# Layer 1's attention beside message passing: values scaled on their way out of PSUM, keys' squares summed by ScalarE, and the step cut in three

## The chip, the cores and the metric

The kernel runs on one core of a Trainium2 chip. The metric is the device time of one execution in microseconds. Three runs of the kernel before took 2911.58, 2914.35 and 2914.36 us; their median is 2914.35 us.

## What is computed

A two-layer graph network on 3125 nodes with 256 features and 50000 edges. Layer 1 adds two branches to x: an edge-softmax message passing, and an attention whose softmax is absent, so that its products can be regrouped. The two branches concerned, cut to what matters and written as plain formulas:

```
xn  = layernorm(x)                                  # 3125 x 256
# branch 1, per edge e = (src, dst), 4 heads of 64
msg = d0[e] * (xn[src] @ Wf.T) + d1[e] * (xn[src] @ Wr.T)      # 64 values
s   = leaky_relu(msg . attn[h], 0.2)                           # 4 scores
out[dst, h] = sum_e softmax_dst(s)[e, h] * msg
# branch 2, 8 heads of 64
k, v = instance_norm(xn @ Wk.T), instance_norm(xn @ Wv.T)      # over each head's 64
out  = (q @ (k.T @ v) / 3125) @ Wout.T + bout
x    = x + branch1 + branch2
```

## The kernel before

`layer1_mix` does branch 1 in a loop over groups of 8 columns of 128 edges: 391 columns, so G = 49 groups, and G + 2 = 51 steps of the loop, numbered i = 0 to 50. The PSUM has eight banks and all are given out: 2 for `ln_pt` (pool `ps_a`), 1 for `pdots`, 4 for `pw` (pool `ps_w`), 1 for `psm`.

What step i issues, in this order:

- `messages(i)` (L1206 to L1217): VectorE weighs the gathered rows by direction, makes scores and their maxima `mx`; TensorE transposes `mx`.
- `weigh(i-1)` (L1263): VectorE multiplies 8 x 4 x 64 message values by the exponentials of the group before. The exponentials lie in column 64 of the tile `v` in SBUF, written by ScalarE (L1238).
- `maximum(i)` (L1224 to L1230): VectorE reduces the transposed maxima, TensorE transposes the new maximum back.
- `products(i-1)` (L1271): TensorE multiplies one-hot matrices with `v`, two or three node tiles of each group, each in a `pw` bank. The profile counts each of these fp32 products as two instructions; there are 14 to 32 of them in a step.
- `add(i-2)` (L1280 to L1287): VectorE adds the products of the group before to `acc`; ScalarE makes the first copy of a node tile.
- `ones_of(i)` (L1255) and `exponents(i)` (L1235 to L1240): one-hot matrices on VectorE, then the subtraction of the maximum and ScalarE's exponentials.
- `next(todo)`: one piece of branch 2, out of the generator `galerkin`.

`galerkin`'s pieces fall on the steps as follows. Step 0 has the weights `wkv`. Steps 1 to 26 have t = 0 to 25: for the tile t-1 VectorE reduces the squares (L1457), forms the product of the variances (L1458, L1460), ScalarE takes its root (L1461), VectorE the reciprocal (L1462), and VectorE scales the values (L1463); TensorE adds keys times values to `pdots` (L1465). Then TensorE makes keys and values of tile t in two `ln_pt` banks (L191), ScalarE copies both out (L1475) and squares both (L1477). Step 27 has `dots` and `woT`, step 28 `m2`, step 29 the matrix `g` and the first chunk of tiles, steps 30 to 35 the other six chunks (L1514, L1515), each of 4 or 3 tiles.

The order is written by hand: TensorE, VectorE and ScalarE run their instructions in the order of the program (`manual_schedule`), each engine waiting on its own for what it needs. GpSimd issues the gathers three groups ahead.

Of the kernel before, what the change touches and what calls it, by code (L numbers as in the profile page):

```python
# [8 lines left out]
F32 = mybir.dt.float32  # L9
I32 = mybir.dt.int32  # L10
BF16 = mybir.dt.bfloat16
AF = mybir.ActivationFunctionType
OP = mybir.AluOpType
AX = mybir.AxisListType
PSUM = bass.MemoryType.PSUM
# [3 lines left out]
D = 256  # L19
P = 125  # L20
# [5 lines left out]
GROUP = 8  # L26
# [23 lines left out]
def gather(nc, out, table, idx):  # L50
    nc.gpsimd.indirect_dma_start(  # L51
        out=out, out_offset=None, in_=table,
        in_offset=bass.IndirectOffsetOnAxis(ap=idx, axis=0))
# [35 lines left out]
class Kernel:  # L89
# [1063 lines left out]
    def layer1_mix(self):  # L1153
        nc, tc, a = self.nc, self.tc, self.a
        W, HD = 68, 64
        with ExitStack() as m:
            big = m.enter_context(tc.tile_pool(name="l1", bufs=1))
            wk = m.enter_context(tc.tile_pool(name="l1w", bufs=2))
            gp = m.enter_context(tc.tile_pool(name="l1g", bufs=3))
            ps_a = m.enter_context(tc.tile_pool(name="l1pa", bufs=2, space=PSUM))  # L1160
            ps_c = m.enter_context(tc.tile_pool(name="l1pc", bufs=1, space=PSUM))
            ps_w = m.enter_context(tc.tile_pool(name="l1pw", bufs=4, space=PSUM))
            ps_s = m.enter_context(tc.tile_pool(name="l1ps", bufs=1, space=PSUM))

            xT = big.tile([128, 2, N], F32, name="xT2")
# [3 lines left out]
            for t0, n in CHUNKS:  # L1169
                st = wk.tile([P, 4, 2 * W], F32, name="t1_st")  # L1170
                for i in range(n):
                    pm = ps_a.tile([P, 2 * W], F32, name="ln_pt")
# [22 lines left out]
            def fetch(j0):  # L1195
                n = min(GROUP, NJ - j0)
                g = gp.tile([128, GROUP, 2 * W], F32, name="g1", bufs=4)
                for i in range(n):
                    gather(nc, g[:, i, :], tab1[:], self.t_src[:, j0 + i:j0 + i + 1])
                return j0, n, g  # L1200
# [32 lines left out]
            def exponents(n, s, pb):  # L1233
                big2 = gp.tile([128, 2, 4], F32, name="top_b", bufs=4)
                nc.vector.tensor_copy(big2, pb)  # L1235
                nc.vector.tensor_sub(s[:, :n, :], s[:, :n, :], big2[:, 0:1, :].to_broadcast([128, n, 4]))
                v = gp.tile([128, GROUP, 4, HD + 1], F32, name="v1", bufs=2)
                nc.scalar.activation(v[:, :n, :, HD], s[:, :n, :], AF.Exp)  # L1238
                grown = gp.tile([128, 4], F32, name="grown", bufs=4)
                nc.scalar.activation(grown, big2[:, 1, :], AF.Exp)  # L1240
                return big2, grown, v

            def tiles_in(j0, n):

# [5 lines left out]
            def ones_of(j0, n):  # L1250

                hots = []
                for w, i0, k in tiles_in(j0, n):
                    hot = gp.tile([128, GROUP, P], F32, name="hot", bufs=5)
                    nc.vector.scalar_tensor_tensor(  # L1255
                        hot[:, :k, :], self.t_dst[:, j0 + i0:j0 + i0 + k, None].to_broadcast([128, k, P]),
                        float(-w * P), self.node[:, None, :P].to_broadcast([128, k, P]),
                        op0=OP.add, op1=OP.is_equal)
                    hots.append(hot)
                return hots  # L1260

            def weigh(n, o, v):
                nc.vector.tensor_mul(v[:, :n, :, :HD], o[:, :n, None, :HD].to_broadcast([128, n, 4, HD]),  # L1263
                                     v[:, :n, :, HD:].to_broadcast([128, n, 4, HD]))

            def products(j0, n, v, hots):
                sums = []
# [23 lines left out]
            with tc.manual_schedule(engines={E_.PE, E_.DVE, E_.Activation}):  # L1291
                todo = self.galerkin(big, wk, ps_a, ps_c, xT)
                starts = [(j0, min(GROUP, NJ - j0)) for j0 in range(0, NJ, GROUP)]
                G = len(starts)
                ahead = [fetch(starts[i][0]) for i in range(3)]
                msg, exps, summed = {}, {}, {}
                for i in range(G + 2):
                    if i + 3 < G:
                        ahead.append(fetch(starts[i + 3][0]))
                    if i < G:  # L1300
                        j0, n, g = ahead[i]
                        o, s, pt = messages(j0, n, g)
                    if 0 <= i - 1 < G:
                        weigh(starts[i - 1][1], msg[i - 1][0], exps[i - 1][2])
                    if i < G:
                        pb = maximum(pt)
                    if 0 <= i - 1 < G:
                        summed[i - 1] = products(*starts[i - 1], exps[i - 1][2], msg[i - 1][1])
                    if 0 <= i - 2 < G:
                        add(*starts[i - 2], *exps[i - 2][:2], summed[i - 2])  # L1310
                    if i < G:
                        msg[i] = o, ones_of(j0, n)
                        exps[i] = exponents(n, s, pb)
                    next(todo, None)
                last = exps[G - 1][0]
# [14 lines left out]
            for t0, n in CHUNKS:  # L1330
                s = slice(t0, t0 + n)
                for t in range(t0, t0 + n):
                    for h in range(4):
                        xs = self.x[:, t, h * HD:(h + 1) * HD]
# [93 lines left out]
    def galerkin(self, big, wk, ps_a, ps_c, xT):  # L1428

        nc, a = self.nc, self.a
        wkv = big.tile([128, 2, 1024], F32, name="wkv")
        for c4 in range(2):
            nat = wk.tile([128, 4, D], F32, name="nat4", bufs=1)
# [16 lines left out]
        kvs = {}  # L1452
        for t in range(NT + 1):
            if t > 0:
                kv, sq = kvs.pop(t - 1)
                var = wk.tile([P, 16], F32, name="kv_var")
                nc.vector.tensor_reduce(var, sq, AX.X, OP.add)  # L1457
                nc.vector.tensor_scalar(var, var, 1.0 / 64, LN_EPS, op0=OP.mult, op1=OP.add)  # L1458
                both = wk.tile([P, 8], F32, name="kv_both")
                nc.vector.tensor_mul(both, var[:, 0:8], var[:, 8:16])  # L1460
                nc.scalar.activation(both, both, AF.Sqrt)  # L1461
                nc.vector.reciprocal(both, both)  # L1462
                nc.vector.tensor_mul(kv[:, 8:, :], kv[:, 8:, :], both[:, :, None].to_broadcast([P, 8, 64]))  # L1463
                for hp in range(4):
                    nc.tensor.matmul(pc[:, hp, :],  # L1465
                                     kv[:, 8 + 2 * hp:10 + 2 * hp, :].rearrange("p a b -> p (a b)"),
                                     kv[:, 2 * hp:2 * hp + 2, :].rearrange("p a b -> p (a b)"),
                                     start=(t == 1 and hp == 0), stop=(t == NT and hp == 3),
                                     skip_group_check=True)
            if t < NT:  # L1470
                kv = wk.tile([P, 16, 64], F32, name="kv")
                for i in range(2):
                    pk = ps_a.tile([P, 512], F32, name="ln_pt")
                    self.token_matmul(pk, xT, t, wkv[:, :, 512 * i:512 * i + 512])
                    nc.scalar.copy(kv[:, 8 * i:8 * i + 8, :].rearrange("p a b -> p (a b)"), pk)  # L1475
                sq = wk.tile([P, 16, 64], F32, name="kv_sq", bufs=1)
                nc.scalar.activation(sq, kv, AF.Square)  # L1477
                kvs[t] = kv, sq
            yield
        dots = big.tile([128, 4, 128], F32, name="dots")  # L1480
        nc.vector.memset(dots, 0.0)
        for s in (slice(0, 64), slice(64, 128)):
            nc.vector.tensor_copy(dots[s, :, s], pc[s, :, s])

        woT = big.tile([128, 4, D], F32, name="woT")
        nat = wk.tile([128, 2, 512], F32, name="nat4", bufs=1)
        nc.sync.dma_start(nat, a["L1_mix_Wout"].rearrange("(c p) f -> p c f", p=128))
        for cc in range(2):
# [2 lines left out]
                nc.tensor.transpose(pt[:, i, :], nat[:, cc, i * 128:(i + 1) * 128], self.ident)  # L1491
            nc.scalar.copy(woT[:, :, cc * 128:(cc + 1) * 128], pt)
        yield
        m2 = big.tile([128, 4, D], F32, name="m2")
        for hp in range(4):
            pm = ps_a.tile([128, D], F32, name="ln_pt")
# [2 lines left out]
        wq = wk.tile([128, 4, D], F32, name="nat4", bufs=1)  # L1499
        nc.sync.dma_start(wq, a["L1_mix_Wqkv"][0:512, :].rearrange("(c p) d -> p c d", p=128))  # L1500
        yield
        g = big.tile([128, 2, D], F32, name="gm")
        for k in range(2):
            pm = ps_a.tile([128, D], F32, name="ln_pt")
            for hp in range(4):
                nc.tensor.matmul(pm, wq[:, hp, k * 128:(k + 1) * 128], m2[:, hp, :],
                                 start=(hp == 0), stop=(hp == 3))
            nc.scalar.copy(g[:, k, :], pm)
        bout = self.bcast(big, "L1_mix_bout")
        for t0, n in CHUNKS:  # L1510
            for t in range(t0, t0 + n):
                pm = ps_a.tile([P, D], F32, name="ln_pt")
                self.token_matmul(pm, xT, t, g)
                nc.vector.tensor_add(self.x[:, t, :], self.x[:, t, :], pm)  # L1514
            nc.vector.tensor_add(self.x[:, t0:t0 + n, :], self.x[:, t0:t0 + n, :],  # L1515
                                 bout[:, None, :].to_broadcast([P, n, D]))
            yield


# [309 lines left out]
```

## Time and profile before

| view | what | value |
|---|---|---|
| runs | median of three | 2914.35 us |
| profiled execution | own time, span | 2909.29 us, 2907.5 us |
| page, part 1 | PE, VectorE, ScalarE, GpSimd busy | 75%, 53%, 17%, 57% of the span |
| windows | steps 2 to 26, 1653.2 to 1957.9 us | 304.7 us: PE 275.7, VectorE 270.8, ScalarE 136.9, GpSimd 242.4 busy; granted clock 0.99 |
| windows | steps 29 to 35, 1986.8 to 2116.9 us | 130.1 us: PE 85.2, VectorE 77.1, ScalarE 4.7, GpSimd 77.9 busy; clock 0.82 |
| windows | steps 36 to 50, 2116.9 to 2246.0 us | 129.1 us: PE 101.2, VectorE 114.0, ScalarE 7.4, GpSimd 86.2 busy; clock 0.87 |

A row of the timeline has the start in us, the duration in us, the engine, the line, the operation, its tiles (out<-in), shapes, a count of merged rows, and in brackets how long the engine sat idle before it and who ended that. PE is a matmul, PEld a weight load, DVE is VectorE, ACT is ScalarE, POOL is GpSimd. A row of a window table has the stretch, its length, and for each engine its busy time with the count of instructions, then the granted clock.

### The profile page before, as it was taken

The numbers are of one execution on the slowest core, as the hardware profiler recorded it, in microseconds if no ns is written. First come the engines' busy times: TensorE is split into PE (matmuls) and PEld (weight loads), VectorE is DVE, ScalarE is ACT, GpSimd is POOL, SyncE is SP. The second block draws the span as 40 slices with busy tenths as digits, with TensorE's granted clock in tenths as the row PEclk, the third lists the DMA queues.
The fourth block names the chain that finished last, engine by engine and source line by source line (L and its number), as shares of the span: only waits on it lengthen the run. The fifth ranks groups of instructions, "written<-read, shape, count | busy, mean of one in ns | idle before, by whom it ended". The sixth has DMA issues, their size and how long they took to land. (4 is left out here: it accounts for less than half of the span.)

```text
span 2907.5 us, 26381 instructions
## 1 busy us (share of the span) xinstructions
PE 2176.8 (75%) x9022; PEld 1642.5 (56%) x9022; DVE 1533.5 (53%) x3540; ACT 503.8 (17%) x1024; POOL 1645.7 (57%) x1489
## 2 busy tenths in 40 slices
PE   1761779999959999999994599886677669992600
PEld 1450557777645668888883466655555546661400
DVE  7975796644679212221115499886588412111337
ACT  2320000000012112222221244440000212220200
POOL 4888887770006316666661677777475077776040
PEclk9865879999959999999996799998888689996855
DMA  8921513342102135555544222222111211221214
GB/s 291 381 78 43 128 41 87 87 107 59 53 30 64 39 122 165 186 185 189 189 151 106 73 49 48 47 48 57 31 42 33 66 15 25 39 46 15 59 48 104
DMA packets 178958, 263.41 MB, mean 91 GB/s; under 512 B 54175, under 2 KB 143753, under 8 KB 175426
## 3 DMA queue, kind: packets, MB, share of 16 engines
q1 hardware_dynamic: 120432, 204.77, 22.8%
q0 software_dynamic: 52480, 47.70, 8.1%
q10 hardware_dynamic: 5894, 9.09, 0.9%
q8 instruction: 75, 1.23, 0.2%
q14 instruction: 77, 0.62, 0.1%
HBM read 177.13 MB, written 84.20 MB: 90 GB/s over the span
## 5 line engine op out<-in xcount | busy, mean ns | idle before, releaser
L58 POOL DMA_INDIRECT adj<-ch_sum,ch_place x391 | 500.3, 1280 | 152.0 <-issue 113.8
L51 POOL DMA_INDIRECT g<-tab,t_src x391 | 458.1, 1172 | 222.6 <-issue 111.9
L58 POOL DMA_INDIRECT sorted<-s_rows,pos x256 | 245.1, 957 | 187.0 <-DVE s_rows L1050 118.4
L460 PE MATMUL psum<-sup,adjT 125*125 125x256 f32 x1250 | 292.3, 394 | 46.6 <-DMA adjT<-adj 34.7
L1271 PE MATMUL pw<-v,hot 128*125 128x260 f32 x1244 | 318.5, 418 | 0.0
L460 PEld LDWEIGHTS psum<-sup,adjT 125*125 125x125 f32 x1250 | 240.3, 194 | 88.2 <-DMA adjT<-adj 25.3
L51 POOL DMA_INDIRECT G<-tabg,g_src x256 | 242.3, 947 | 80.0 <-issue 71.6
L1271 PEld LDWEIGHTS pw<-v,hot 128*125 128x125 f32 x1244 | 252.3, 206 | 47.3
L1626 PE MATMUL fpy<-fw,fh 128*125 128x256 f32 x800 | 183.4, 388 | 79.3 <-DVE fy L1628 52.7
L859 PE MATMUL ph<-xs,w 128*128 128x256 f32 x1024 | 231.3, 385 | 8.4 <-issue 6.8
L887 PE MATMUL py<-w,h 128*128 128x256 f32 x1024 | 231.2, 380 | 0.0
L859 PEld LDWEIGHTS ph<-xs,w 128*128 128x128 f32 x1024 | 193.9, 192 | 45.2 <-issue 18.6
L1626 PEld LDWEIGHTS fpy<-fw,fh 128*125 128x125 f32 x800 | 153.1, 192 | 112.6 <-DVE fy L1628 53.1
L887 PEld LDWEIGHTS py<-w,h 128*128 128x128 f32 x1024 | 192.5, 190 | 24.6
L861 ACT ACTIVATE h<-ph,b 128x256 f32<-128x256 f32 x256 | 121.2, 474 | 366.0 <-PE ph L859 336.5
L1618 PE MATMUL fph<-xT,fw 128*128 128x500 f32 (+1 forms) x448 | 174.5, 541 | 0.3 <-DMA fb<-in_L_ffn_b_dram 0.3
L1025 PE MATMUL pctx<-s_mv,s_ro 128*128 128x256 f32 x512 | 155.1, 414 | 1.9 <-DVE s_mv L1024 1.9
L1620 ACT ACTIVATE fh<-fph,cols 128x500 f32<-128x500 f32 (+1 forms) x112 | 70.6, 633 | 364.3 <-PE fph L1618 329.5
L890 DVE TENSOR_SCALAR yo<-py,own 128x256 f32<-128x256 f32 x64 | 29.6, 480 | 193.9 <-PE py L887 193.9
L58 POOL DMA_INDIRECT slots<-rows,abi x50 | 72.8, 1456 | 100.0 <-DVE r_cum L939 85.1
L463 DVE TENSOR_TENSOR x<-x,psum 125x512 f32<-125x512 f32 (+1 forms) x104 | 68.8, 664 | 108.9 <-PE psum L460 108.8
L1618 PEld LDWEIGHTS fph<-xT,fw 128*128 128x128 f32 x448 | 85.0, 191 | 72.6 <-issue 49.8
(495 smaller groups left out, 3241.2 us busy)
## 6 DMA issues: line engine op xcount, KB each, us to landing
adjT<-adj SPq DMA_DIRECT2D x25, 1367.2 KB
adj<-zero SPq DMA_DIRECT2D x22, 1536.0 KB
w<-in_L_ffn_W1p_dram SPq DMA_DIRECT2D x32, 1024.0 KB
w<-in_L_ffn_W2p_dram SPq DMA_DIRECT2D x32, 1024.0 KB
slots<-empty SPq DMA_DIRECT2D x1, 8448.0 KB
srow<-slots SPq DMA_DIRECT2D x32, 264.0 KB
adj<-ch_sum,ch_place POOLq DMA_INDIRECT x391, 4.4
g<-tab,t_src POOLq DMA_INDIRECT x391, 2.6
```

The lines of the kernel that those rows point to most:

```text
L51: nc.gpsimd.indirect_dma_start(out=out, out_offset=None, in_=table, in_offset=bass.IndirectOffsetOnAxis(ap=idx, axis=0))
L58: return nc.gpsimd.indirect_dma_start(out=table, out_offset=bass.IndirectOffsetOnAxis(ap=idx, axis=0), in_=rows, in_offset=None, **kw)
L460: nc.tensor.matmul(pm[:, i, :], mats[b][:, (a0 + i) * P:(a0 + i + 1) * P], sup[:, b, :], start=(b == b0), stop=(b == b0 + n - 1))
L463: nc.vector.tensor_add(xs, xs, pm[:, :m, :])
L859: nc.tensor.matmul(ph, w1[:, k, f * 128:(f + 1) * 128], xs[:, k, :], start=(k == 0), stop=(k == 1))
L861: nc.scalar.activation(h[:, f, :], ph, AF.Gelu, bias=b1[:, f:f + 1])
L887: nc.tensor.matmul(py, h[:, f, i * 128:(i + 1) * 128], w2[:, f, :], start=(f == 0), stop=(f == FC - 1))
L1025: nc.tensor.matmul(p1, ro[:, f - f0, :], mv, **st)
L1271: nc.tensor.matmul(pw.rearrange("p h c -> p (h c)"), hot[:, i - i0, :], v[:, i, :, :].rearrange("p h c -> p (h c)"), start=(i == i0), stop ...
L1618: nc.tensor.matmul(ph[:, :n * P], w1[:, k, f * 128:(f + 1) * 128], xT[:, k, t0 * P:(t0 + n) * P], start=(k == 0), stop=(k == 1))
L1620: nc.scalar.activation(hs[:, f, :n * P], ph[:, :n * P], AF.Gelu, bias=self.col("L1_ffn_b1", ei * FC + f))
L1626: nc.tensor.matmul(py, hs[:, f, i * P:(i + 1) * P], w2[:, f, :], start=(f == 0), stop=(f == FC - 1))
```

## The change

- `ScalarE` writes the exponentials twice: into a new PSUM tile `ev`, from which `weigh` reads them, and into `v` as before. `ev` takes one bank, so `pw` has 3 instead of 4.
- `galerkin`'s tile loop is cut in three by `yield`, and a step of the outer loop calls `next(todo)` three times: ahead of `messages`, ahead of `maximum`, and at the end. The first part holds the reduction of the squares up to the root, the second the reciprocal and the scaling, the third the products and the next tile's keys and values. The other pieces of `galerkin` are padded with empty parts so that they stay in their steps; `dots` comes in the first part of step 27.
- The values stay in PSUM; ScalarE scales them in eight copies by `both`. The keys' squares are summed by ScalarE in eight instructions with `accum_out`; the values are squared out of PSUM in one, and VectorE reduces 512 numbers instead of 1024.
- `bout` is a row added by a product with a row of ones, and two tiles are added to x at a time.

```diff
-            ps_w = m.enter_context(tc.tile_pool(name="l1pw", bufs=4, space=PSUM))
+            ps_w = m.enter_context(tc.tile_pool(name="l1pw", bufs=3, space=PSUM))
+            ps_e = m.enter_context(tc.tile_pool(name="l1pe", bufs=1, space=PSUM))
...
+                ev = ps_e.tile([128, GROUP, 4], F32, name="ev")
+                nc.scalar.activation(ev[:, :n, :], s[:, :n, :], AF.Exp)
                 nc.scalar.activation(v[:, :n, :, HD], s[:, :n, :], AF.Exp)
...
-                                     v[:, :n, :, HD:].to_broadcast([128, n, 4, HD]))
+                                     ev[:, :n, :, None].to_broadcast([128, n, 4, HD]))
...
+                    next(todo, None)
                     if i < G:
                         j0, n, g = ahead[i]
                         o, s, pt = messages(j0, n, g)
                     if 0 <= i - 1 < G:
-                        weigh(starts[i - 1][1], msg[i - 1][0], exps[i - 1][2])
+                        weigh(starts[i - 1][1], msg[i - 1][0], *exps[i - 1][2:])
+                    next(todo, None)
                     if i < G:
                         pb = maximum(pt)
...
+        yield
+        yield
         wkv = big.tile([128, 2, 1024], F32, name="wkv")
...
             if t > 0:
-                kv, sq = kvs.pop(t - 1)
-                var = wk.tile([P, 16], F32, name="kv_var")
-                nc.vector.tensor_reduce(var, sq, AX.X, OP.add)
+                kv, pv, var, sq = kvs.pop(t - 1)
+                nc.vector.tensor_reduce(var[:, 8:], sq, AX.X, OP.add)
...
                 nc.scalar.activation(both, both, AF.Sqrt)
+            yield
+            if t > 0:
+
                 nc.vector.reciprocal(both, both)
-                nc.vector.tensor_mul(kv[:, 8:, :], kv[:, 8:, :], both[:, :, None].to_broadcast([P, 8, 64]))
+                for h in range(8):
+                    nc.scalar.activation(kv[:, 8 + h, :], pv[:, 64 * h:64 * h + 64], AF.Copy,
+                                         scale=both[:, h:h + 1])
+            yield
+            if t > 0:
                 for hp in range(4):
...
             if t < NT:
                 kv = wk.tile([P, 16, 64], F32, name="kv")
-                for i in range(2):
-                    pk = ps_a.tile([P, 512], F32, name="ln_pt")
-                    self.token_matmul(pk, xT, t, wkv[:, :, 512 * i:512 * i + 512])
-                    nc.scalar.copy(kv[:, 8 * i:8 * i + 8, :].rearrange("p a b -> p (a b)"), pk)
-                sq = wk.tile([P, 16, 64], F32, name="kv_sq", bufs=1)
-                nc.scalar.activation(sq, kv, AF.Square)
-                kvs[t] = kv, sq
...
+                pk = ps_a.tile([P, 512], F32, name="ln_pt")
+                self.token_matmul(pk, xT, t, wkv[:, :, :512])
+                pv = ps_a.tile([P, 512], F32, name="ln_pt")
+                self.token_matmul(pv, xT, t, wkv[:, :, 512:])
+                for h in range(8):
+                    nc.scalar.activation(junk, pk[:, 64 * h:64 * h + 64], AF.Square,
+                                         accum_out=var[:, h:h + 1])
+                nc.scalar.copy(kv[:, :8, :].rearrange("p a b -> p (a b)"), pk)
+                nc.scalar.activation(sq.rearrange("p a b -> p (a b)"), pv, AF.Square)
+                kvs[t] = kv, pv, var, sq
             yield
...
         for t0, n in CHUNKS:
-            for t in range(t0, t0 + n):
-                pm = ps_a.tile([P, D], F32, name="ln_pt")
-                self.token_matmul(pm, xT, t, g)
-                nc.vector.tensor_add(self.x[:, t, :], self.x[:, t, :], pm)
-            nc.vector.tensor_add(self.x[:, t0:t0 + n, :], self.x[:, t0:t0 + n, :],
-                                 bout[:, None, :].to_broadcast([P, n, D]))
+            for t1 in range(t0, t0 + n, 2):
+                m = min(2, t0 + n - t1)
+                pm = ps_a.tile([P, 2, D], F32, name="ln_pt")
+                for i in range(m):
+                    for k in range(2):
+                        nc.tensor.matmul(pm[:, i, :], xT[:, k, (t1 + i) * P:(t1 + i + 1) * P], g[:, k, :],
+                                         start=(k == 0), stop=False)
+                    nc.tensor.matmul(pm[:, i, :], self.full[0:1, :P], bout, start=False, stop=True)
+                xs = self.x[:, t1:t1 + m, :]
+                nc.vector.tensor_add(xs, xs, pm[:, :m, :])
+            yield
+            yield
             yield
```

## The prediction, made before the changed kernel ran

> **What bounds the kernel now.** The page's busy shares are a mean over many stages, so I went straight to the windows of the loop of layer 1, the only code touched, and then to its timeline.
>
> ```profile
> core 0: us, PE busy (x) PEld busy (x) DVE busy (x) ACT busy (x) POOL busy (x), PEclk, DMA share, GB/s
> 1653.20:1957.90 304.70, 275.71 (x1121) 188.83 (x1120) 270.82 (x530) 136.91 (x228) 242.42 (x205) 0.99 0.21 47
> 1986.80:2116.90 130.10, 85.19 (x313) 67.27 (x313) 77.14 (x146) 4.67 (x23) 77.87 (x71) 0.82 0.17 39
> 1974.50:1978.00 3.50, 3.50 (x9) 2.77 (x9) 2.24 (x6) 0.41 (x3) 2.68 (x3) 0.50 0.26 60
> ```
>
> Row 1 (steps 2 to 26, with the keys and values) takes 12.2 us a step with TensorE 90% and VectorE 89% busy: two engines in balance, working on different pieces at once. Row 2 (steps 29 to 35, the chunks) takes 18.6 us a step though both engines have less to do: there they take turns. Row 3 is explained below. The timeline of step 15 shows how the balance is made:
>
> ```profile
> 1801.67 6.84 PE L1271 MATMUL pw<-v,hot 128*125 128x260 f32 x30
> 1804.72 1.21 DVE L1457 TENSOR_REDUCE kv_var<-kv_sq 125x16 f32<-125x1024 f32 x1
> 1806.72 0.20 DVE L1462 RECIPROCAL kv_both<-kv_both 125x8 f32<-125x8 f32 x1 [0.38 <-ACT kv_both L1461]
> 1807.57 0.72 DVE L1206 TENSOR_TENSOR msg<-g,t_dir 128x544 f32<-128x544 f32 x1
> 1808.34 1.06 PE L1465 MATMUL pdots<-kv 125*128 125x128 f32 x8
> 1809.24 3.60 PE L191 MATMUL ln_pt<-wkv,xT 128*125 128x512 f32 x8
> 1811.15 0.59 ACT L1475 COPY kv<-ln_pt 125x512 f32<-125x512 f32 x1 [4.47 <-PE ln_pt L191]
> 1812.87 0.59 ACT L1475 COPY kv<-ln_pt 125x512 f32<-125x512 f32 x1 [1.13 <-PE ln_pt L191]
> 1813.49 1.06 ACT L1477 ACTIVATE kv_sq<-kv 125x1024 f32<-125x1024 f32 x1
> 1816.91 1.21 DVE L1457 TENSOR_REDUCE kv_var<-kv_sq 125x16 f32<-125x1024 f32 x1
> ```
>
> TensorE starts a step's products in the middle of VectorE's step and is still at that step's keys and values when VectorE has begun the next one (L1206 at 1807.57). The squares of that tile end at 1814.55, and VectorE asks for them only at 1816.91, the end of the next step. That slack of 2.4 us is all that keeps VectorE from waiting for TensorE here. A chunk step has no such slack: VectorE adds in the same piece in which TensorE multiplies.
>
> ```profile
> 2050.95 8.67 PE L1271 MATMUL pw<-v,hot 128*125 128x260 f32 x30
> 2059.46 3.62 PE L191 MATMUL ln_pt<-gm,xT 128*125 128x256 f32 x16
> 2060.52 0.42 DVE L1514 TENSOR_TENSOR x<-x,ln_pt 125x256 f32<-125x256 f32 x1 [7.13 <-PE ln_pt L191]
> 2064.71 0.72 DVE L1206 TENSOR_TENSOR msg<-g,t_dir 128x544 f32<-128x544 f32 x1
> 2067.21 2.28 DVE L1263 TENSOR_TENSOR v<-msg,v 128x2048 f32<-128x2048 f32 x1
> 2069.41 0.27 DVE L1224 TENSOR_REDUCE top<-psm 4x1 f32<-4x128 f32 x1
> ```
>
> VectorE idles 7.13 us for TensorE, then TensorE idles until the next products at 2070.29: 19.3 us.
>
> **What the Trainium skill says.** (1) "TensorE: Matmul & The Clock Gate", Part 1: after an idle window of about 3.4 us the array runs at half clock, and needs about as long of sustained work to get back. The trace agrees: the third window row shows a granted clock of 0.50 in the first 3.5 us of products after an idle stretch, and 30 products take 8.51 us in a chunk step (2050.95 to 2059.46) against 6.67 (1801.67 to 1808.34). (2) "ScalarE: Activation LUTs", What ACT_TABLE_LOAD costs: 186 ns + 0.833 ns an element, 93 ns more for a pointer scale, and neighbours overlap by 93 ns. The 125x512 copy at 586 ns (613 by this) agrees roughly. (3) "VectorE: DVE perf modes", The perf-mode tier table: an fp32 tensor_tensor runs one element a cycle from SBUF and from PSUM alike, 2293 ns for 2048; L1263's mean is 2293. (4) "SBUF — State Buffer", Who interferes with whom: a VectorE instruction with two SBUF inputs contends with GpSimd's reads. Under L1263 a gather lasts 1.90 us (1811.29) against 0.94 elsewhere, which fits.
>
> **The change part by part.**
>
> *VectorE's work* falls each step: the reduce has 512 instead of 1024 elements (1.21 us at 1.04 ns an element, so 0.53 less), L1463 goes (0.61 from its start to the next), the wait for the root goes (0.38). That is 1.5 us a step, 38 us over 25 steps, if VectorE's work stayed the bound.
>
> *The place of the reduce.* It moves from the end of step i+1 to its start, and is the first thing after the third part of step i, which makes the very squares it reads. Ahead of it VectorE would stand at 1804.72 in the trace above, and the squares are there at 1814.55: 9.8 us late. Queued behind it on VectorE are messages, weigh and maximum, and TensorE's next products wait for the maximum. So the steps become turns, like the chunk steps. I count one turn from the start of products to the next:
>
> - products: 634 instructions in these 25 turns (from the tile bounds in the code), 25.4 a turn at 6.67/30 = 0.222 us: 5.64
> - half clock at their start: TensorE will idle some 7.5 us, as in the chunk steps. Excess over 0.222 each: 1.84 (30 instructions), 2.43 (22, from 2070.29 to 2077.61), 2.50 (32, from 1974.51 to 1984.12), 2.15 (20, from 1992.37 to 1998.96). I take 2.2
> - `pdots`, 1808.34 to 1809.24: 0.90. Keys, to ScalarE's start: 1.91
> - ScalarE from the keys on: eight squares with their accumulator reads. L609's pair (256 elements) goes from start to start in 0.40 us; 192 elements fewer at 0.833 ns give 0.24, times 8 is 1.92. The copy of the keys 0.50, the square of the values 0.60 (values are ready 1.72 after the keys, in time). Together 3.02
> - hand-over 0.05, reduce 0.72, two small operations 0.31: 1.08
> - messages, 1807.57 to 1810.06: 2.49. Weigh, 2067.21 to 2069.41: 2.20. Reciprocal, now here: 0.15. Maximum, 2069.41 to the products at 2070.29: 0.88
>
> The sum is 20.5 us. Now the 25 turns take 301.7 us (products at 1651.11 to products at 1952.78), then 511: **+210 us**.
>
> *Step 27.* `dots` at its start waits for `pdots` of step 26 in the same way. Turn 26 now is 10.6 (1952.78 to 1963.41); then 7.11 + 2.2 + 1.0 + 0.86 (the copies) + 2.49 + 2.20 + 0.88 = 16.7: +6.1. Turn 27 loses the 1.4 us of `dots`. Together +4.7.
>
> *Chunks.* A bias product is two instructions at 0.215 us (16 of the L191 kind take 3.45 from start to start): 0.43 a tile, with TensorE already the one waited for. Four tiles: 4 x 1.29, a hand-over of 0.2 and the last paired add, 0.62, is 5.98 against 5.25 (2059.46 to 2064.71). Three: 4.4 against 4.1. Four and three times: +3.8.
>
> *At nothing:* the eight scaled copies. By (2) 186 + 93 + 53 - 93 = 0.24 each, 1.9 together (0.13 each, by the overlap alone, is the low end); they begin at the maximum and must be done before `pdots`, 8.7 us later; without that cover they would cost 1.9 a turn. The second exponential (0.26) and both table loads (1.28 each; the root's load begins when the squares end, and the reciprocal comes some 5 us later): ScalarE is idle then. Weights from PSUM: L1282 with a PSUM input takes 425 ns against 416 for L1280, so -0.1 to +0.1 a step; I take nothing. GpSimd gets shorter gathers, but with turns of 20 us it waits for buffers anyway. Three `pw` banks: the first adds run beside the first products, so 0 to 0.3 a step; I take nothing. `bout` as one row: loaded long ahead.
>
> **The sum.** 2909.29 + 210 + 4.7 + 3.8 = 3127.8 for the profiled execution. The median of the runs is 5.1 higher than that execution, so 3132.9; I say 3130.
>
> **The rivals.**
>
> (B) *TensorE stays warm.* The same turns without the 2.2 us: 55 less, 3075. For it: the clock was 0.99 in these steps. Against: it was 0.82 in the chunk steps, whose idle gaps are as long.
>
> (C) *Accumulator reads don't overlap.* L609's rows add up to 0.42 - 0.16 + 0.19 = 0.45 for 64 elements, 0.21 more than I count: 8 x 25 x 0.21 = 42 more, 3172. The trace shows overlap for 256 elements; for 64 it shows nothing.
>
> (D) *The squares are there in time, and the kernel gets faster.* Place: the wait ahead of the reduce. If TensorE and ScalarE finished tile t before VectorE asks, VectorE's saving of 38 us would stand against the 8.5 of `dots` and chunks: about 2885. It decides at 1.5 us of waiting a step; above that the change loses. For it: ScalarE idles 4.47 us before the keys. Against: what it idles for is TensorE, and the trace has the squares 9.8 us behind the new place of the reduce.
>
> (E) *The change does not do what it says*, if the order of the program is not the order of the engines. VectorE's rows follow the program line by line now, so this is small; it would give about 2914.
>
> **Chances.** Forecast 0.78, own range 3095 to 3165 (ScalarE's pairs from 0.20 to 0.30, the cold start from 1.8 to 2.6, banks and weights as bounded, some 0.5 us a turn for hand-overs I cannot see). B 0.07, C 0.10, D 0.04, E 0.01. The range takes in the forecast's whole range and C: 3085 to 3180. About 0.2% can be told from no change here. Faster 0.04 (D), same 0.01 (E), slower 0.95.
>
> **What would show it.** After: 25 turns of about 20 us where there were 12; VectorE idle 8 to 10 us ahead of the reduce of `kv_var`, ended by ScalarE's squares; TensorE idle over 7 us a step and a granted clock of about 0.8 in place of 0.99; `messages` right behind the reduce; L1514's successor adding two tiles in 0.68 us; later steps as before. I am wrong if the reduce does not wait (D), if the pairs are not 0.24 us from start to start (C), or if products after the gap run at 0.222 each (B).

## The result, and the profile after

The changed kernel took 3161.36 us (median of four runs, 3160.41 to 3162.64), the kernel before 2913.69 us beside it: a ratio of 1.0858, 95% interval 1.0845 to 1.0871. It is slower by 248 us. Forecast were 3130 us and a range of 3085 to 3180.

I cut both traces at the start of each step's products, as in the prediction, and took the differences:

| products of step ... to step ... | before, us | after, us | difference |
|---|---|---|---|
| 1 to 26 (25 turns with keys and values) | 301.7 | 540.7 | +239.1 |
| 26 to 27 (`dots` at the start) | 10.6 | 17.3 | +6.7 |
| 27 to 29 (`woT`, `m2`) | 28.9 | 25.0 | -4.0 |
| 29 to 36 (chunks) | 130.2 | 141.6 | +11.5 |
| 36 to 48 (branch 1 alone) | 112.0 | 112.3 | +0.4 |

They add up to 253.6 (the differences are taken before rounding); the profiled executions (2909.29 and 3162.64 us) differ by 253.4. What lies ahead of these steps differs by +1.8 us and what lies behind them by -2.1, so the loss is in the loop. The window of the 25 turns, before and after:

```profile
core 0: us, PE busy (x) PEld busy (x) DVE busy (x) ACT busy (x) POOL busy (x), PEclk, DMA share, GB/s
1651.10:1952.80 301.70, 272.71 (x1103) 186.11 (x1102) 268.06 (x523) 132.93 (x221) 240.24 (x202) 0.98 0.21 47
1652.90:2193.60 540.70, 329.87 (x1102) 226.73 (x1101) 238.57 (x503) 213.84 (x820) 222.76 (x218) 0.77 0.11 28
```

VectorE works 239 us in the 25 turns where it had 268, as the change meant it to. But its share falls from 89% to 44%, TensorE's from 90% to 61%, and the granted clock from 0.98 to 0.77. Both engines wait; the list of waits of that window says for whom (total, times, longest):

```profile
DVE kv_var L1463 <- ACT kv_sq L1496: 288.5, 25, 13.7
PE psm L1218 <- DVE mx L1216: 154.7, 25, 6.5
```

All 25 reduces wait for the squares, 11.5 us each. One turn in the timeline after, beside the rows of step 15 before:

```profile
1873.89 3.60 PE L191 MATMUL ln_pt<-wkv,xT 128*125 128x512 f32 x8
1875.87 0.22 ACT L1493 ACTIVATE kv_junk<-ln_pt 125x64 f32<-125x64 f32 x1 [7.31 <-PE ln_pt L191]
1875.99 0.20 ACT L1493 ACTIVATION_READ_ACCUMULATOR kv_junk<-ln_pt 125x1 f32 x1
1876.21 0.23 ACT L1493 ACTIVATE kv_junk<-ln_pt 125x64 f32<-125x64 f32 x1
...
1878.51 0.58 ACT L1495 COPY kv<-ln_pt 125x512 f32<-125x512 f32 x1
1878.97 0.61 ACT L1496 ACTIVATE kv_sq<-ln_pt 125x512 f32<-125x512 f32 x1
...
1879.62 0.69 DVE L1463 TENSOR_REDUCE kv_var<-kv_sq 125x8 f32<-125x512 f32 x1 [11.54 <-ACT kv_sq L1496]
...
1880.92 0.73 DVE L1207 TENSOR_TENSOR msg<-g,t_dir 128x544 f32<-128x544 f32 x1 [0.21 <-issue]
...
1883.65 0.37 PE L1218 MATMUL psm<-ident,mx 128*4 128x128 f32 x1 [6.17 <-DVE mx L1216]
...
1886.57 9.34 PE L1274 MATMUL pw<-v,hot 128*125 128x260 f32 x30
```

Read it from top to bottom: keys on TensorE, squares on ScalarE, reduce and messages on VectorE, and only then TensorE again. In these rows no engine works beside another for long (the keys' squares run beside the values' products, the one-hot matrices beside the products at the end). Before, the messages (L1206 at 1807.57) began 7 us ahead of the end of these squares (1814.55).

### The profile page after: what moved, and what is told of

The parts are those of the page before. It is cut to its first block, busy times and chain, and to the rows that moved or that the text cites. A ratio compares the mean times of both kernels' runs of the same rounds, so it can differ in the third digit from the quotient of the medians.

```text
span 3160.8 us, 27099 instructions
## 1 busy us (share of the span) xinstructions
PE 2255.2 (71%) x9072; PEld 1689.4 (53%) x9072; DVE 1488.5 (47%) x3497; ACT 585.5 (19%) x1648; POOL 1603.4 (51%) x1489
## 5 line engine op out<-in xcount | busy, mean ns | idle before, releaser
L51 POOL DMA_INDIRECT g<-tab,t_src x391 | 404.3, 1034 | 518.9 <-DVE score L1211 339.4
L58 POOL DMA_INDIRECT adj<-ch_sum,ch_place x391 | 510.8, 1306 | 149.4 <-issue 112.4
L1274 PE MATMUL pw<-v,hot 128*125 128x260 f32 x1244 | 376.0, 472 | 1.9 <-DVE acc L1285 1.9
L1274 PEld LDWEIGHTS pw<-v,hot 128*125 128x125 f32 x1244 | 292.0, 239 | 67.2 <-issue 2.6
L1658 PEld LDWEIGHTS fpy<-fw,fh 128*125 128x125 f32 x800 | 153.9, 193 | 112.0 <-DVE fy L1660 53.5
L1218 PE MATMUL psm<-ident,mx 128*4 128x128 f32 x49 | 16.7, 340 | 213.8 <-DVE mx L1216 213.8
L1463 DVE TENSOR_REDUCE kv_var<-kv_sq 125x8 f32<-125x512 f32 x25 | 17.1, 686 | 288.5 <-ACT kv_sq L1496 288.5
```

The source lines that it names most:

```text
L51: nc.gpsimd.indirect_dma_start(out=out, out_offset=None, in_=table, in_offset=bass.IndirectOffsetOnAxis(ap=idx, axis=0))
L58: return nc.gpsimd.indirect_dma_start(out=table, out_offset=bass.IndirectOffsetOnAxis(ap=idx, axis=0), in_=rows, in_offset=None, **kw)
L1218: nc.tensor.transpose(pt, mx, self.ident)
L1274: nc.tensor.matmul(pw.rearrange("p h c -> p (h c)"), hot[:, i - i0, :], v[:, i, :, :].rearrange("p h c -> p (h c)"), start=(i == i0), stop ...
L1658: nc.tensor.matmul(py, hs[:, f, i * P:(i + 1) * P], w2[:, f, :], start=(f == 0), stop=(f == FC - 1))
```

## The experiments

Turn lengths are means of the 25 turns from products of step 1 to products of step 26, out of each profile: 12.07 us before, 21.63 after.

### The reduce back at the end of the step, everything else kept (e1_end)

```diff
         for t in range(NT + 1):
+            yield
+            yield
             if t > 0:
                 kv, pv, var, sq = kvs.pop(t - 1)
...
                 nc.scalar.activation(both, both, AF.Sqrt)
-            yield
-            if t > 0:
                 nc.vector.reciprocal(both, both)
...
-            yield
-            if t > 0:
                 for hp in range(4):
```

> The whole change, but the reduce, the root, the reciprocal and the scaled copies stand at the end of the step, ahead of the products with the values, where they stood before. Theory (the place of the reduce, directly behind the squares it reads, makes the loss): the turns fall from 21.6 us to about 12, limited by TensorE; what is left over the kernel before is the chunks (about 8) and dots (about 3): 2915 to 2930 us. Rival 1 (ScalarE's 24 small instructions a step make the loss): nothing changes in them, so 3140 to 3160. Rival 2 (three banks for pw, weights out of PSUM): the same, 3140 to 3160.

Measured: 2931.18 us, ratio 1.0067 (1.0050 to 1.0083). The turn is 12.43 us. Of the 239 us that the turns had lost, 230 are gone with nothing but the order changed; rivals 1 and 2, which put the loss into the work or the banks, fall. What remains is the chunks (142.8 against 130.2) and 0.36 us a turn. TensorE's rows say where these 0.36 us sit; a step's `pdots` before, and the same one in e1_end:

```profile
1796.12 1.13 PE L1465 MATMUL pdots<-kv 125*128 125x128 f32 x8 [0.95 <-DVE kv L1463]
1801.20 1.72 PE L1475 MATMUL pdots<-kv 125*128 125x128 f32 x8 [0.81 <-ACT kv L1472]
```

It begins as soon as the first two heads are scaled, but then its four products, of two heads each, come 0.41 us apart, in step with ScalarE's eight copies. From the start of `pdots` to that of the keys it is 1.31 us on the mean, where it was 0.95.

VectorE works 241 us in these turns, 27 less than before, and gains nothing by it. The trace of e1_end at the end of a step shows what VectorE waits for now:

```profile
1810.31 0.19 DVE L1237 TENSOR_TENSOR score<-score,top_b 128x32 f32<-128x32 f32 x1
1810.42 0.68 DVE L1465 TENSOR_REDUCE kv_var<-kv_sq 125x8 f32<-125x512 f32 x1
...
1811.00 1.28 ACT L1469 ACT_TABLE_LOAD   x1
...
1812.30 0.21 ACT L1469 ACTIVATE kv_both<-kv_both 125x8 f32<-125x8 f32 x1
1812.54 0.20 DVE L1470 RECIPROCAL kv_both<-kv_both 125x8 f32<-125x8 f32 x1 [1.01 <-ACT kv_both L1469]
```

The exponentials and the load of the table of roots (ACT_TABLE_LOAD, 1.28 us) lie between the scores and the root. From the start of the reduce to the reciprocal it is 2.12 us (1810.42 to 1812.54), and it was 2.00 before (1804.72 to 1806.72), though the reduce is 0.53 us shorter. VectorE's wait for the root grew from 9.0 us in all to 24.1, and its wait for the transposed maxima (TensorE's turn) from 14.4 to 33.5.

### The cut alone, on the kernel before (e2_split)

```diff
+                    next(todo, None)
                     if i < G:
                         j0, n, g = ahead[i]
...
                 nc.scalar.activation(both, both, AF.Sqrt)
+            yield
+            if t > 0:
                 nc.vector.reciprocal(both, both)
                 nc.vector.tensor_mul(kv[:, 8:, :], kv[:, 8:, :], both[:, :, None].to_broadcast([P, 8, 64]))
+            yield
+            if t > 0:
                 for hp in range(4):
...
```

> The kernel before with the step cut in three alone: reduce to root at the start of the step, reciprocal and L1463 ahead of the maximum, the rest at the end; no work is added or taken away, dots stays where it was. Theory: 25 turns, each products 5.6 + half clock 2.4 + pdots 0.9 + keys 1.95 + values, copy and square 3.4 + reduce and product 1.75 + messages and weigh 4.7 + reciprocal and scaling 0.85 + maximum 0.83 = 22.4 us against 12.1: 3150 to 3180 us. Rivals 1 and 2: about 2914.

Measured: 3161.85 us, ratio 1.0865 (1.0847 to 1.0883), a turn of 22.13 us. Cutting the step makes the whole loss, with no work added or taken away. Its list of waits has the same first row:

```profile
DVE kv_var L1461 <- ACT kv_sq L1485: 269.6, 25, 12.8
```

### The reduce in the middle of the step (e5_mid, e5b_mid)

```diff
         for t in range(NT + 1):
+            yield
             if t > 0:
                 kv, pv, var, sq = kvs.pop(t - 1)
...
-            yield
-            if t > 0:
                 for hp in range(4):
```

> The changed kernel with the reduce to the root between weigh and maximum, and reciprocal and scaled copies at the end of the step. Theory: messages and weigh (4.7 us) now run while VectorE would have waited, and the idle stretch of TensorE is shorter, so that less of it is at half clock: products 5.6 + pdots 0.9 + keys 2.0 + ScalarE 3.75 + reduce and product 1.3 + maximum 0.83 = 14.4, up to 16.8 with half clock: 2980 to 3045 us, between the two other places. Rivals that put the loss elsewhere: 3140 to 3160.

> The kernel of e5_mid again, because the chip of that run was slower for the kernel before too. Turns of 14.4 to 16.8 us as counted: 2980 to 3045 us.

e5_mid, e6_weights, e7_bias and e8_best ran on another chip, on which the kernel before took 3283.57 us; their traces show single stops in these steps, up to 36 us long, that the profile puts down to "remote". So these four are told by their ratio to the kernel before on that chip, and e5b_mid and e6b_weights are two of them on a chip that ran the kernel before in 2910.78 us. e5_mid: 1.0547 (1.0491 to 1.0604). e5b_mid: 3040.93 us, 1.0448 (1.0432 to 1.0464), a turn of 16.64 us. So the same work gives 21.63, 16.64 and 12.43 us a turn with the reduce at the start, in the middle and at the end: the loss follows the place. In e5b_mid the reduces wait 167.1 us in all, 6.7 each.

### TensorE kept busy in the gap (e3_filler, e3b_filler2)

```diff
                 self.token_matmul(pv, xT, t, wkv[:, :, 512:])
+                fill = ps_e.tile([128, D], F32, name="fill")
+                for r in range(13):
+                    nc.tensor.matmul(fill, self.ident, wkv[:, 0, :D], start=True, stop=True)
...
```

> The changed kernel with the weights read from SBUF again, and the freed bank used for 13 products (26 instructions) of the identity with the weights of keys and values, which nobody reads, behind the values' products of each of the steps 1 to 25. They fill about 5.6 of the 6.2 us in which TensorE idles ahead of the transposition of the maxima, and are no part of the result. If half clock after the idle stretch costs 2.4 us a turn: 25 times 2.4 less, 3095 to 3110 us, granted clock near 1 in the turns. If the clock is no cause: 3155 to 3170.

Measured: 3150.57 us, ratio 1.0827 (1.0809 to 1.0845), a turn of 21.24: a miss. Its trace shows two of 24 turns with products at the full rate; in the others they begin at half clock, as in the changed kernel. One of these:

```profile
1848.04 5.77 PE L1492 MATMUL fill<-wkv,ident 128*128 128x256 f32 x26
1854.38 0.27 PE L1218 MATMUL psm<-ident,mx 128*4 128x128 f32 x1 [0.56 <-DVE mx L1216]
1856.92 0.44 PE L1231 MATMUL psm<-ident,top 4*128 4x4 f32 x2 [2.28 <-DVE top L1226]
1857.30 7.99 PE L1272 MATMUL pw<-v,hot 128*125 128x260 f32 x22
```

Of the 3.5 us between the fill and the products TensorE idles 2.8, broken by two short transpositions (not 2.4 of 3.2, as I put it below). Gaps of 3.4 to 4.2 us cost the clock in 22 turns; in the two others the gap was 3.4 us too. So the gap was filled further:

```diff
                 nc.tensor.transpose(pt, mx, self.ident)
+                if fills:
+                    for r in range(4):
+                        nc.tensor.matmul(fills[-1][0], self.ident, fills[-1][1], start=True, stop=True)
                 return o, s, pt
...
```

> e3_filler with four more idle products behind the transposition of the maxima, so that the array has work in all but about 1 us ahead of the products (in e3_filler it still idled some 2.4 us of the last 3.2, and most turns began at half clock again). Nobody reads what they write. If half clock is worth 2.4 us a turn: 25 times 2.4 less than the changed kernel, 3095 to 3110 us, clock near 1. If the array still falls back: 3145 to 3155.

Measured: 3106.97 us, ratio 1.0676 (1.0659 to 1.0692), a turn of 19.38, clock 1.00 in the turns. TensorE's rows in e3b_filler2:

```profile
1864.45 0.27 PE L1219 MATMUL psm<-ident,mx 128*4 128x128 f32 x1 [0.55 <-DVE mx L1217]
1864.56 1.89 PE L1222 MATMUL fill<-wkv,ident 128*128 128x256 f32 x8
1867.00 0.40 PE L1235 MATMUL psm<-ident,top 4*128 4x4 f32 x2 [0.55 <-DVE top L1230]
1867.32 6.84 PE L1276 MATMUL pw<-v,hot 128*125 128x260 f32 x30
```

Thirty products take 6.68 us to the next row, the rate of before. Half clock is thus worth 2.25 us of the 9.6 us that a turn lost, 56 us in all. The other 7.3 us stay at the full clock: half clock adds to the waiting, and does not make it.

### The keys squared in one instruction (e4_onesq)

```diff
-                for h in range(8):
-                    nc.scalar.activation(junk, pk[:, 64 * h:64 * h + 64], AF.Square,
-                                         accum_out=var[:, h:h + 1])
+                nc.scalar.activation(sq[:, :8, :].rearrange("p a b -> p (a b)"), pk, AF.Square)
...
```

> The changed kernel with the keys squared in one instruction out of PSUM and all 1024 squares reduced by VectorE: no accumulator reads. On the path of a turn ScalarE needs 2.36 us from the keys on instead of 3.75, VectorE 0.53 more: 0.86 less a turn, 3135 to 3145 us. Rival 1 (ScalarE's small instructions are the loss): half or more of it goes, under 3050.

Measured: 3128.46 us, ratio 1.0754 (1.0736 to 1.0772), a turn of 20.32: 1.31 less, and I had expected 0.86. ScalarE needs 2.35 us from the keys on instead of 3.75, and VectorE 0.53 more, as counted. The rest is TensorE's clock: behind a shorter gap the products take 7.69 us a turn (the 24 turns with `pdots`), against 8.10 in the changed kernel. The sums by ScalarE thus make things worse, but by a seventh of the loss.

### Weights from PSUM alone (e6_weights, e6b_weights)

The diff's lines on `ps_w`, `ps_e`, `ev` and `weigh`, put on the kernel before.

> The kernel before with the weights read from PSUM alone (a bank for ev, three for pw). My count: -0.1 to +0.3 us in each of 49 steps, 2909 to 2929 us. Rival 2: a loss of 100 us or more. Shorter gathers under weigh in any case, near 0.94 us in place of 1.9.

> The kernel of e6_weights again, for the same reason. 0 to 0.3 us in each of 49 steps: 2910 to 2925 us; gathers under weigh near 0.94 us.

e6_weights: ratio 1.0108 (1.0073 to 1.0143), on the slower chip. e6b_weights: 2912.28 us, 1.0004 (0.9998 to 1.0011), no change that can be told. The gathers of steps 2 to 26, 1191 ns on the mean before, take 1021 ns in e6b_weights, since those that start under the weighing no longer take longer than the rest (0.94 us on the mean, against 2.06 before); but VectorE's list of waits before has no wait for a gather in these steps. The third bank that `pw` lost shows as well: TensorE waits ahead of products three times, 2.0 us in all, and never in the kernel before. The loss on the other chip need not come from the change: of the 39 us by which e6_weights exceeds the kernel before in the 25 turns, 35 lie in the first two of them, beside stops put down to "remote". The kernel before was not traced on that chip, so this stays open.

### Bias by product alone (e7_bias)

The diff's last part, put on the kernel before.

> The kernel before with the bias by product and two tiles an add alone. As counted ahead of the result: +3.8 us, 2918. By the profile after (a tile every 1.67 us instead of 0.86 with the adds beside): 7 to 12 us more, 2921 to 2926.

Measured: ratio 1.0034 (1.0009 to 1.0058), on the slower chip; 0.34% of 2914 us is 10 us. Its own trace has 163.3 us in the chunks, 141.6 without one "remote" stop of 21.7. The other traces confirm it: the chunks take 130.2 to 130.6 us in the kernels without it (before, e2_split, e6b_weights, e9_keysum) and 141.4 to 142.8 in those with it (after, e1_end, e3_filler, e3b_filler2, e4_onesq, e5b_mid).

### Keys' sums alone, and all but order and bias (e9_keysum, e8_best)

e9_keysum puts the eight squares with `accum_out` and the reduce of 512 numbers on the kernel before, with copy and scaling of the values as they were. e8_best is e1_end with the bias and the place of `dots` of before.

> The kernel before with one part of the change alone: ScalarE sums the keys' squares out of PSUM in eight instructions, VectorE reduces the values' 512 squares at the old place. VectorE has 0.53 us a step less to do, ScalarE ends its squares about 1 us later, still ahead of the reduce. If VectorE is what limits a step: up to 13 us less, 2897 to 2905. If TensorE is: 2907 to 2914.

> The whole change less its order and its bias: reduce to scaled copies at the end of the step as before, dots at the end of step 27, bias added by VectorE; values scaled out of PSUM, keys' squares summed by ScalarE and weights from PSUM stay. VectorE has 1.1 us a step less to do, but TensorE is busy 90% of these steps, so at most 0.5 us of it can show: 2895 to 2916 us. If TensorE's own order sets the step: no gain.

e9_keysum: 2912.22 us, 1.0007 (0.9998 to 1.0015), no gain from 0.53 us a step less on VectorE. What it saves goes into the wait found in e1_end; this row stood at 9.0 us before:

```profile
DVE kv_both L1461 <- ACT kv_both L1460: 23.7, 24, 1.3
```

TensorE's waits in the 25 turns say how much there was to gain. The first two rows are from the kernel before, the third from e9_keysum:

```profile
PE pdots L1465 <- DVE kv L1463: 15.1, 12, 2.3
PE psm L1230 <- DVE top L1225: 13.8, 25, 0.6
PE pdots L1464 <- DVE kv L1462: 17.0, 12, 2.3
```

Before, TensorE is busy for 272.7 of the 301.7 us, and these two waits are the rest. The second is the hand-over of the maximum, 0.55 us in every turn. The first is what less work on VectorE could shorten, and it occurs in 12 turns only. In the twelve turns whose products are 26 instructions or more TensorE does not wait for VectorE ahead of `pdots` at all: a turn with 32 takes 12.6 us before, in e1_end and in e9_keysum alike. And where TensorE waits, it waits for values that wait for the root.

e8_best: 1.0122 (1.0085 to 1.0160), on the slower chip. Its trace, too, has the "remote" stops in the first two turns; its other 23 turns take 291.8 us, against 282.2 in e7_bias, which has the code of before in these turns. It is no gain either, and its size is not told. No version here beats the kernel before.

## Why the prediction was right, and where its sizes were off

The mechanism was right: the reduce waits for the squares just made, the engines take turns, and the clock falls. (The wait of the reduce is 11.5 us, and not the 8 to 10 named as its sign: the 9.8 was read in a step at full clock.) e1_end and e2_split show the place of the reduce to be the cause; D is out, since the reduce never found its squares ready, and E too. B is out by the clock of 0.77, and e3b_filler2 gives the 2.2 us that B would have saved as 2.25. C was half right. Term by term, per turn, with the means of the 25 turns after:

| term | predicted, us | measured, us |
|---|---|---|
| products, with half clock | 7.84 | 7.99 |
| `pdots`; keys to ScalarE's start | 0.90; 1.91 | 0.86; 1.99 |
| eight squares with their sums | 1.92 | 2.64 |
| copy and values' square | 1.10 | 1.11 |
| hand-over, reduce, two operations | 1.08 | 1.32 |
| messages, weigh | 2.49, 2.20 | 2.50, 2.19 |
| reciprocal, maximum | 0.15, 0.88 | 0.11, 0.92 |
| sum | 20.47 | 21.63 |

The mis-sized term is the pair of square and accumulator read: 0.34 us from start to start (1875.87 to 1876.21), not 0.24. I had taken L609's 0.40 and subtracted the elements; but the rows show that the read (0.20) now has a gap of some 0.02 us behind it before the next square, where L609's next square begins 0.1 us ahead of the read's end. That is 0.72 us a turn, 18 of the 30 us by which the turns exceed my +210. Another 6 are the small operations (VectorE stands 0.2 us ahead of the messages for nothing the trace names), and 4 the half clock. Two more are a term that I had put at nothing, the three `pw` banks: in three turns TensorE waits 0.6 us for one ahead of the products (1.9 us in all), as in e1_end, e4_onesq and e6b_weights with their three banks, and never before, in e2_split or in e9_keysum with four. The eight scaled copies, also put at nothing, do cost nothing here: they take 1.75 us and end some 7 us ahead of `pdots`. In e1_end, where that cover is gone, they show.

The second term off is the bias. I priced a product at 0.215 us, and the chunks at +3.8; they cost +11.5. The timeline of a chunk after:

```profile
2267.98 1.03 PE L1542 MATMUL ln_pt<-gm,xT 128*125 128x256 f32 x4
2268.94 0.69 PE L1544 MATMUL ln_pt<-bout,full 1*125 1x256 f32 x2
2269.56 1.13 PE L1542 MATMUL ln_pt<-gm,xT 128*125 128x256 f32 x4
2270.62 0.69 PE L1544 MATMUL ln_pt<-bout,full 1*125 1x256 f32 x2
2271.24 1.13 PE L1542 MATMUL ln_pt<-gm,xT 128*125 128x256 f32 x4
```

A tile follows the last in 1.58 to 1.68 us, against 0.86 before, not 1.29: the pair of the bias holds TensorE for 0.62, and the tile's own four products take some 0.1 to 0.2 us longer. Half clock it is not: the granted clock is 1.00 in these rows. Why a product with one row takes this long stays open. The trace of before had such a pair, L812 (nine rows by 256), but I took my rate from a run of like products. `dots` at +6.7 and the shorter turn behind it at -1.5 were near the count (+6.1, -1.4); that `m2` then comes 2.5 us sooner I had not seen. That the weights from PSUM and the second exponential cost next to nothing held: 112.3 against 112.0 us for the last 12 turns.

That the total fell inside 3085 to 3180 is in part luck. A pair of 0.344 us lies outside the 0.20 to 0.30 that I had allowed it, and the bias had no range of its own. The large misses all went one way, and the top of the range had been set by rival C, which came half true.

## What to carry to other kernels

In a loop written by hand, ask of each reader how far behind its writer it stands, in work of its own engine: here 2.4 us of slack kept two engines side by side, and moving one reduce by less than a step turned 12 us into 22. A cut that only reorders can cost more than all the work it is to spread, so test the order alone. And before taking work off a busy engine, look at what it would wait for next, and whether the other engine waits for it at all: here the root came no sooner, since a table load stands ahead of it, and in every second turn TensorE had no wait for VectorE left to shorten. What the kernel would gain without that table load was not tried.

## What the runs showed of the hardware

Three things I had not expected. A stretch of 3.4 to 4.2 us in which TensorE did only two short transpositions brought half clock in 22 of 24 turns, although 5.8 us of full work lay just ahead of it (e3_filler); with 1.2 us of idling or less there, in e3b_filler2, the clock stayed at 1.00. A square of 64 elements with its accumulator read takes 0.34 us, so that eight of them (2.64 us) take over four times as long as one square of all 512 out of PSUM (0.60). And a product with a single row, bracketed by products with 128, lengthened a tile by 0.8 us (0.86 to 1.67), about as much as the tile itself took.
